# The first stage's scatter matmuls: one 128x128 matmul per slot tile instead of four in column groups of 32

## The chip, the cores and the metric

One core of one Trainium2 chip. The metric is the device time of one execution in microseconds (us). The kernel before has a median of 5328.8 us over 8 runs, from 5324.69 to 5338.14. One of its executions was profiled, and every duration below is from that execution.

## The reference, cut to what matters

A graph with 12,500 nodes of 96 features and 200,000 edges goes through four residual layers, each followed by a layer norm. The first layer is the one whose stage is changed:

```python
def _L0_gnn_ref(x, src, dst, W_self, W_neigh, b):
    n = x.shape[0]
    msg = x[src]
    neigh_sum = jax.ops.segment_sum(msg, dst, num_segments=n)
    deg = jax.ops.segment_sum(jnp.ones(src.shape, x.dtype), dst, num_segments=n)
    h_neigh = neigh_sum / jnp.maximum(deg, 1.0)[:, None]
    return x @ W_self + h_neigh @ W_neigh + b
...
x = _layernorm(x + _L0_gnn_ref(x, src, dst, L0_gnn_W_self, L0_gnn_W_neigh, L0_gnn_b), axis=-1)
x = _layernorm(x + _L1_gnn_ref(...), axis=-1)   # two rounds of the same kind of segment sum
x = _layernorm(x + _L2_gnn_ref(...), axis=-1)   # attention over the edges
x = _layernorm(x + _L3_gnn_ref(...), axis=-1)   # softmax-weighted segment sum
```

`dst` is sorted. The work that matters here is `msg = x[src]` followed by `segment_sum` over `dst`: a gather and a scatter-add.

## The kernel before, in words

Nodes are handled in 98 blocks of 128. Gather and scatter are both matmuls with one-hot matrices in fp8. For the first 76 blocks (`NS`), the edges that end in block `d` are placed in 25 *slot tiles* (`SQ`) of 128 slots. Every slot tile goes through three steps in `first_sums`:

- **gather** (L1302): four matmuls, each with 32 columns of the one-hot matrix `ohT` as weights and 192 columns of the node table (two f16 halves of 96 features) moving. Each fills one group of 32 partitions of `rows` in PSUM. They stay four in both kernels, because the four groups read different pieces of the table.
- **copy** (L1306): ScalarE turns `rows` into f16 `msg`, two or four slot tiles at a time (1 or 2 PSUM banks, alternating).
- **scatter** (L1316): `msg`, now 194 columns with a column of ones that counts the degree, is multiplied by the one-hot matrix `ohd` and added up in `acc`. 25 slot tiles end in one `acc`, which VectorE reduces (L1496).

A gather runs one group ahead of its scatter. `ohT` of a block is built from its broadcast row `bc` by VectorE (L1224) for even blocks and by ScalarE (L1221 and L1222) for odd blocks, and `ohd` by VectorE (L1206 and L1210). Both have two buffers, so those of block `d` wait until TensorE is through with block `d - 2`.

In the first stage (`passes`) this is interleaved with the bucketing of the edges (`edge_block` and `edge_steps`), which finds each edge's slot. Its steps are VectorE work (L1071 to L1087 for the counts, L1099 to L1133 for the ranks, L1142 to L1159 for the one-hot matrices `A` and `R`), with TensorE matmuls between them: L1089, L1102 and L1103, and L1166, which places 128 edges a time in `place`. ScalarE copies `place` (L1174), `expand` makes the block's rows of it (L1181, a transpose L1183, L1185), and DMAs broadcast them. The remaining 22 blocks are summed by `by_edges`, whose one-hot matrices `ones_e` (L1368) meet gathered rows in L1373. Nodes that are finished go through `l0_stage` (transposes L748, matmuls L1527).

In this stage the order of instructions on each engine is not the program's text: a scheduler sets it when the kernel is built, from what it takes each instruction to cost. Each engine then runs its own list strictly in that order. The later sums over slot tiles (`whole_pass`) have the same two steps as L1444 and L1455, and there the scatter of the second layer is one 128x128 matmul of 192 columns, while that of the fourth layer is four of 32 columns each, 384 columns long.

Of the kernel before, what the change touches and what calls it, by code (L numbers as in the profile page):

```python
# [23 lines left out]
P = 128  # L24
# [491 lines left out]
GR = 32  # L516
NG = 4
SQ = 25
# [24 lines left out]
def gnn_fast(  # L543
# [4 lines left out]
    nc = tc.nc  # L548
# [226 lines left out]
    def advance():  # L775
        if pending and next(pending[0], pending) is pending:
            pending.pop(0)
# [400 lines left out]
    def expand(work, psum, placed, d):  # L1178

        lo = work.tile([P, 2 * SQ + 1], F32, name="lo", bufs=5)  # L1180
        nc.vector.tensor_add(lo, placed[d][:, 1], placed[d + 1][:, 0])  # L1181
        p = psum.tile([SQ, P], F32, name="tp")
        nc.tensor.transpose(p, lo[:, :SQ], ident)  # L1183
        r = work.tile([SQ, P], BF16, name="lorow", bufs=2)
        nc.scalar.copy(r, p)  # L1185
        nc.scalar.dma_start(rowd[d], r)

        s = work.tile([SPARE, 1], F32, name="s_", bufs=2)
        nc.vector.scalar_tensor_tensor(
            s, lo[:SPARE, SQ : SQ + 1], float(P), lo[:SPARE, SQ - 1 : SQ], op0=ALU.mult, op1=ALU.add  # L1190
        )
        nc.vector.tensor_scalar(spare_i[:, d : d + 1], s, -1.0, 0.0, op0=ALU.add, op1=ALU.max)
        h = d % 2 * SPARE
        nc.scalar.dma_start(spare_2[h : h + SPARE, d // 2 : d // 2 + 1], spare_i[:, d : d + 1])
        return lo[:, SQ + 1 :]

    def ask_row(work, d):
        bc = work.tile([P, SD], BF16, name="bc", bufs=2)
        nc.sync.dma_start(bc, rowd[d].rearrange("q p -> (q p)")[None, :].to_broadcast([P, SD]))
        return bc  # L1200

    def destinations(work, d, lo):

        ohd = work.tile([P, SQ, P], FP8, name="ohd", bufs=2)
        by = ohd.rearrange("p q e -> p (q e)").bitcast(I32).rearrange("p (q w) -> p q w", q=SQ)
        nc.vector.scalar_tensor_tensor(  # L1206
            by, lo[:, :, None].to_broadcast([P, SQ, WQ]), 8.0, word[:, None, :].to_broadcast([P, SQ, WQ]),
            op0=ALU.mult, op1=ALU.subtract,
        )
        nc.vector.tensor_tensor(by, one8[:, None, :].to_broadcast([P, SQ, WQ]), by, op=ALU.logical_shift_left)  # L1210
        nc.sync.dma_start(ohd_d[d], ohd.rearrange("p q e -> p (q e)"))
        return ohd

    def one_hots(work, d, bc):

        o = work.tile([P, SD], FP8, name="ohT0", bufs=2)
        if d % 2:

            for c in range(0, SD, SD // 2):
                b = bc[:, c : c + SD // 2]  # L1220
                nc.scalar.activation(b, b, AF.Square, bias=less)  # L1221
                nc.scalar.activation(o[:, c : c + SD // 2], b, AF.Relu, bias=1.0, scale=-1.0, saturate=False)  # L1222
        else:
            nc.vector.tensor_scalar(o, bc, pcol1, None, op0=ALU.is_equal, saturate=False)  # L1224
        nc.sync.dma_start(ohT_d[d], o)
        return o
# [15 lines left out]
    def gather_spare(table, d):  # L1242
        ring = spare["ring"]
        t = ring[d % len(ring)]
        nc.gpsimd.indirect_dma_start(  # L1245
            out=t[:SPARE, : table.shape[1]], out_offset=None, in_=table,
            in_offset=bass.IndirectOffsetOnAxis(ap=spare_i[:, d : d + 1], axis=0),
        )
        return t
# [10 lines left out]
    def granule(at, ohs, sp, q, j, half=0):  # L1260

        if q == SQ - 1 and j < 2:
            c = half * SPARE + j * GR
            return ident_h[:, c : c + GR], sp
        s = NG * q + j - (2 if q == SQ - 1 else 0)
        return ohs[:, q * P + j * GR : q * P + (j + 1) * GR], at(s)

    AHEAD = 3
    def first_sums(work, msgp, psum, at, table, placed, done):


        W = 2 * D
        R = 2

        msgs = {}
        for banks in (1, 2):
            msgs[banks] = [msgp.tile([P, R * banks, 2, D + 1], F16, name=f"msg{banks}_{i}", bufs=1) for i in range(3)]
            for m in msgs[banks]:
                nc.gpsimd.memset(m[:, :, 0, D:], 1.0)
                nc.gpsimd.memset(m[:, :, 1, D:], 0.0)  # L1280
        got, acc, rowed, made = {}, {}, {}, {}

        def fetch(d):

            if d < NS - 2:
                made[d + 2] = expand(work, psum, placed, d + 2)
            if 0 <= d + 1 < NS:
                rowed[d + 1] = ask_row(work, d + 1)
            if 0 <= d < NS:
                got[d] = (  # L1290
                    one_hots(work, d, rowed.pop(d)), destinations(work, d, made.pop(d)), gather_spare(table, d)
                )

        def gather(now, banks):
            ps = psum.tile([P, banks, 512], F32, name=f"rows{banks}")
            m = msgs[banks].pop(0)
            msgs[banks].append(m)
            for i, (d, q) in enumerate(now):
                ohs, _, sp = got[d]
                for j in range(NG):  # L1300
                    a, b = granule(at, ohs, sp, q, j)
                    nc.tensor.matmul(  # L1302
                        ps[j * GR : (j + 1) * GR, i // R, i % R * W : (i % R + 1) * W], a, b, start=True, stop=True
                    )
            n = -(-len(now) // R)
            nc.scalar.copy(  # L1306
                m[:, : n * R].rearrange("p (b r) t w -> p b (r t) w", r=R)[:, :, :, :D],
                ps[:, :n, : R * W].rearrange("p b (t w) -> p b t w", w=D),
            )
            return [(d, q, m[:, i].rearrange("p t w -> p (t w)")) for i, (d, q) in enumerate(now)]  # L1310

        def scatter(d, q, m):
            if q == 0:
                acc[d] = psum.tile([P, 512], F32, name="acc", bufs=2)
            for j in range(0, P, GR):
                nc.tensor.matmul(  # L1316
                    acc[d][j : j + GR, : W + 2], got[d][1][:, q, j : j + GR], m, start=(q == 0), stop=(q == SQ - 1)
                )
            if q == SQ - 1:
                done(work, psum, d, acc.pop(d))  # L1320
                got.pop(d)

        for d in range(1 - AHEAD, 1):
            yield
            fetch(d)
        items = [(d, q) for d in range(NS) for q in range(SQ)]
        waiting, u, banks = [], 0, 2
        while u < len(items):
            now = items[u : u + R * banks]
            for d, q in now:  # L1330
                if q == 0:
                    yield
                    fetch(d + 1)
            waiting.append(gather(now, banks))
            u += R * banks
            banks = 3 - banks
            if len(waiting) > 1:
                for w in waiting.pop(0):
                    scatter(*w)
            advance()  # L1340
        for ws in waiting:
            for w in ws:
                scatter(*w)
# [648 lines left out]
```

## Time and profile before

| | |
|---|---|
| profiled execution | 5326.96 us; span of its instructions 5325.0 us |
| busy over the span | DVE 4158.7 us (78%), PE 4057.6 (76%), POOL 3476.8 (65%), ACT 2792.7 (52%) |
| first stage's scatters, L1316 | 7600 matmuls from 236.4 to 1270.9 us, 345.85 us busy |
| first stage's gathers, L1302 | 7600 matmuls from 230.2 to 1269.4 us |
| mean granted TensorE clock | 0.781; 0.85 in the first stage, 0.94 in the second layer's |

DVE is VectorE, ACT ScalarE, POOL GpSimd, PE TensorE, and PEld its weight loads, which lie beside the matmuls. Overlapping matmuls count once in busy time, so 7600 matmuls of 279 ns each can be busy for 345.85 us. A line such as "A L1142 <- PE place L1166" in the list of waits says that the instruction writing `A` at line 1142 stood idle until TensorE had finished an instruction that writes `place` at line 1166.

### The profile page before, as it was taken

How to read it: one execution, taken by the hardware profiler on the slowest of the kernel's cores; microseconds unless marked ns; L12 is line 12 of the kernel's file. 1: busy time of each engine (PE TensorE's matmuls, PEld its weight loads, DVE VectorE, ACT ScalarE, POOL GpSimd, SP SyncE). 2: the span in 40 equal slices, each digit the busy share in tenths (PEclk: the TensorE clock that was granted, in tenths of full speed). 3: DMA queues.
4: the chain of work that ended last, by engine and by line, in shares of the span. 5: the costliest groups of instructions: out<-in, count | busy, mean ns of one | idle time of the engine just before them, and what ended most of it. 6: DMA issues, size and time to landing. Idle time of an engine off the chain costs nothing. (4 is left out here: it accounts for less than half of the span.)

```text
span 5325.0 us, 155826 instructions
## 1 busy us (share of the span) xinstructions
PE 4057.6 (76%) x63527; PEld 3248.9 (61%) x63527; DVE 4158.7 (78%) x9827; ACT 2792.7 (52%) x5549; POOL 3476.8 (65%) x3338
## 2 busy tenths in 40 slices
PE   3677777776799889995666666766666667999997
PEld 2556666565677667774655655656656565566665
DVE  7689999994567667875888888888888887777776
ACT  1566666665455445553545455454554544555554
POOL 0276667662777477755777777777777776776661
PEclk9688888888899899995565556555565656999999
DMA  3566666656667577765555555555555554555552
GB/s 93 174 207 201 209 219 203 213 176 192 159 188 192 153 193 208 217 190 148 156 158 159 159 160 157 160 159 158 162 158 161 159 157 135 157 156 145 149 151 66
DMA packets 656950, 894.03 MB, mean 168 GB/s; under 512 B 394162, under 2 KB 458885, under 8 KB 651357
## 3 DMA queue, kind: packets, MB, share of 16 engines
q1 hardware_dynamic: 498742, 615.02, 37.1%
q0 software_dynamic: 138784, 262.63, 20.8%
q8 instruction: 500, 8.19, 0.6%
q10 hardware_dynamic: 18695, 6.32, 0.6%
q14 instruction: 229, 1.88, 0.1%
HBM read 747.72 MB, written 135.87 MB: 166 GB/s over the span
## 5 line engine op out<-in xcount | busy, mean ns | idle before, releaser
L1631 POOL DMA_INDIRECT kv<-kv_d,cols x1563 | 1548.4, 991 | 484.9 <-issue 379.0
L1389 POOL DMA_INDIRECT rows_e<-tab_d,cols x1065 | 1232.1, 1157 | 418.5 <-issue 249.6
L1447 ACT CAST msg<-rows 128x384 f16<-128x384 f32 (+1 forms) x1440 | 866.1, 641 | 637.0 <-PE rows L1444 620.5
L1725 PE MATMUL acc<-mh,ohe 128*128 128x208 f16 x2727 | 515.0, 357 | 653.7 <-DVE ohe L1709 648.7
L1447 DVE CAST msg<-rows 128x768 f16<-128x768 f32 x720 | 686.0, 953 | 331.1 <-PE rows L1444 324.8
L1444 PE MATMUL rows<-tab,ohT 128*32 128x192 f16 (+1 forms) x21560 | 796.3, 276 | 67.9 <-DVE msg L1447 35.2
L1725 PEld LDWEIGHTS <-ohe 128*128 128x128 bf16 x2727 | 306.0, 127 | 797.9 <-DVE ohe L1709 736.3
L1455 PE MATMUL acc<-msg,ohd 128*32 128x384 f16 (+1 forms) x10600 | 744.1, 300 | 7.8 <-DVE msg L1447 6.9
L1669 PE MATMUL ep<-w_e,attr 97*128 97x96 f32 x3126 | 701.8, 401 | 5.9 <-DVE s L1677 5.1
L1669 PEld LDWEIGHTS ep<-w_e,attr 97*128 97x128 f32 x3126 | 670.5, 315 | 14.4 <-DVE s L1677 5.5
L1444 PEld LDWEIGHTS <-ohT 128*32 128x32 fp8e4 x21560 | 505.5, 97 | 278.1 <-issue 204.2
L1389 POOL DMA_INDIRECT rows_e<-ex_d,cols x483 | 465.2, 963 | 203.7 <-issue 121.9
L1455 PEld LDWEIGHTS <-ohd 128*32 128x32 fp8e4 (+1 forms) x10600 | 498.5, 98 | 157.2 <-issue 74.3
L1689 ACT ACTIVATE ex<-sc 128x32 f32<-128x32 f32 x391 | 89.6, 229 | 943.4 <-DVE sc L1681 926.1
L1306 ACT CAST msg<-rows 128x768 f16<-128x768 f32 x633 | 382.0, 644 | 188.4 <-PE rows L1302 173.2
L1316 PE MATMUL acc<-msg,ohd 128*32 128x194 f16 x7600 | 345.9, 279 | 157.4 <-ACT msg L1306 155.3
L1677 DVE TENSOR_TENSOR s<-ep,kv 128x384 f32<-128x384 f32 x391 | 217.3, 556 | 317.5 <-DMA kv<-kv_d,cols 273.7
L1709 DVE TENSOR_SCALAR ohe<-wide,within 128x256 bf16<-128x256 bf16 x1563 | 361.3, 312 | 0.0
L1373 PE MATMUL acc<-rows_e,ones_e 128*128 128x192 f16 (+2 forms) x2644 | 332.1, 276 | 30.2 <-DMA rows_e<-tab_d,cols 13.1
L1316 PEld LDWEIGHTS <-ohd 128*32 128x32 fp8e4 x7600 | 209.3, 106 | 220.1 <-issue 205.3
L1302 PE MATMUL rows<-tab,ohT 128*32 128x192 f16 x7448 | 336.0, 275 | 5.4 <-issue 5.4
L1245 POOL DMA_INDIRECT spare<-tab_d,spare_i x76 | 116.0, 1527 | 327.9 <-DMA rowd<-lorow 177.2
(695 smaller groups left out, 7235.1 us busy)
## 6 DMA issues: line engine op xcount, KB each, us to landing
ohT<-ohT_d SPq DMA_DIRECT2D x220, 400.0 KB
ohd<-ohd_d SPq DMA_DIRECT2D x220, 400.0 KB
attr<-cols_edge_attr_dram SPq DMA_DIRECT2D x390, 192.0 KB
bc<-rowd SPq DMA_DIRECT2D x76, 800.0 KB
qb<-qrow SPq DMA_DIRECT2D x97, 512.0 KB
sb<-srow SPq DMA_DIRECT2D x38, 1024.0 KB
ohd_d<-ohd SPq DMA_DIRECT2D x76, 400.0 KB
ohT_d<-ohT SPq DMA_DIRECT2D x76, 400.0 KB
```

Source lines behind the costliest of these rows:

```text
L1302: nc.tensor.matmul(ps[j * GR : (j + 1) * GR, i // R, i % R * W : (i % R + 1) * W], a, b, start=True, stop=True)
L1306: nc.scalar.copy(m[:, : n * R].rearrange("p (b r) t w -> p b (r t) w", r=R)[:, :, :, :D], ps[:, :n, : R * W].rearrange("p b (t w) -> p b t ...
L1316: nc.tensor.matmul(acc[d][j : j + GR, : W + 2], got[d][1][:, q, j : j + GR], m, start=(q == 0), stop=(q == SQ - 1))
L1373: nc.tensor.matmul(acc[:, : W + count], ones[:, :, i], rows_of[u][:, t % UE + i, : W + count], start=(t + i == first), stop=(t + i == last),)
L1389: nc.gpsimd.indirect_dma_start(out=m[:, i, :W], out_offset=None, in_=table, in_offset=bass.IndirectOffsetOnAxis(ap=rest_src[:, t : t + 1], ...
L1444: nc.tensor.matmul(ps[j * GR : (j + 1) * GR, i // R, i % R * W : (i % R + 1) * W], a, b, start=True, stop=True)
L1447: (nc.scalar.copy if engine else nc.vector.tensor_copy)(m, ps[:, :, : R * W])
L1455: nc.tensor.matmul(acc[d][j : j + wide, :W], got[d][1][:, q, j : j + wide], m, start=(q == 0), stop=(q == SQ - 1))
L1631: nc.gpsimd.indirect_dma_start(out=kv[:, i, :], out_offset=None, in_=kv_d, in_offset=bass.IndirectOffsetOnAxis(ap=cols[:, t0 + i : t0 + i ...
L1669: nc.tensor.matmul(ep[:, i, :], a[:, i * P : (i + 1) * P], w_e, start=True, stop=True)
L1709: nc.vector.tensor_scalar(o[:, i], wide, within[:, t0 + i : t0 + i + 1], None, op0=ALU.is_equal)
L1725: nc.tensor.matmul(acc[d].rearrange("p t w -> p (t w)"), ohe[:, i, k * P : (k + 1) * P], m[:, i].rearrange("p t w -> p (t w)"), start=(t = ...
```

## The change

Each slot tile's four scatter matmuls, one for each group of 32 columns of `ohd`, become one matmul with all 128 columns. The operands and the sums are the same.

```diff
         def scatter(d, q, m):
             if q == 0:
                 acc[d] = psum.tile([P, 512], F32, name="acc", bufs=2)
-            for j in range(0, P, GR):
-                nc.tensor.matmul(
-                    acc[d][j : j + GR, : W + 2], got[d][1][:, q, j : j + GR], m, start=(q == 0), stop=(q == SQ - 1)
-                )
+            nc.tensor.matmul(acc[d][:, : W + 2], got[d][1][:, q, :], m, start=(q == 0), stop=(q == SQ - 1))
             if q == SQ - 1:
                 done(work, psum, d, acc.pop(d))
                 got.pop(d)
```

## The prediction

> **What bounds the kernel now.** I read the table of windows first, to find the stage that the change touches, then who waits for whom inside it, then single matmuls on the timeline. The columns of the windows are PE, PEld, DVE, ACT and POOL busy (with instructions), granted clock, DMA share and GB/s.
>
> ```profile
> core 0: us, PE busy (x) PEld busy (x) DVE busy (x) ACT busy (x) POOL busy (x), PEclk, DMA share, GB/s
> 230.00:400.00 170.00, 111.33 (x2760) 89.81 (x2758) 140.28 (x282) 104.37 (x155) 131.67 (x93) 0.80 0.69 220
> 400.00:600.00 200.00, 158.68 (x3650) 125.80 (x3651) 188.18 (x411) 133.94 (x220) 130.48 (x89) 0.88 0.65 206
> 600.00:800.00 200.00, 152.98 (x3576) 120.40 (x3569) 189.57 (x431) 128.63 (x206) 127.72 (x86) 0.85 0.66 212
> 800.00:1000.00 200.00, 153.78 (x3603) 122.21 (x3603) 189.73 (x406) 129.38 (x212) 140.46 (x86) 0.85 0.64 201
> 1000.00:1272.00 272.00, 202.12 (x4808) 161.65 (x4807) 211.13 (x473) 180.55 (x294) 130.16 (x80) 0.85 0.58 190
> ...
> 1200.00:1250.00 50.00, 35.23 (x948) 27.94 (x949) 20.13 (x41) 38.46 (x64) 6.76 (x4) 0.86 0.73 237
> ```
>
> From 400 to 1000 us DVE is busy 567.5 of 600 us, 94.6%; PE is at 77.6%, ACT at 65%. VectorE sets the pace there. From about 1200 us it does not: 20 of 50 us busy, and what is left is a tail of gathers, copies and scatters to 1271 us. So the change can act in two ways: through DVE's waits for TensorE, and through the length of the tail. Those waits, from 230 to 1200 us:
>
> ```profile
> DVE ohT L1224 <- PE rows L1302: 15.3, 8, 8.9
> DVE A L1142 <- PE place L1166: 9.4, 13, 1.8
> ...
> DVE ones_e L1368 <- PE acc L1373: 7.1, 13, 1.3
> ...
> DVE ohd L1206 <- PE acc L1316: 5.7, 5, 3.9
> ```
>
> The columns are total us, times, longest. With three smaller rows (2.3, 1.6 and twice 0.5) DVE waits 42.4 us for PE.
>
> **The matmuls themselves.** The change takes away 7600 matmuls and weight loads and adds 1900, which is certain from the built program. What array time is that? The timeline has both forms back to back: four column groups in the first stage (first two lines and the start of the third), and 128x128 scatters between 128x32 gathers in the second layer. Columns: start, us, what.
>
> ```profile
> 709.25 0.52 PE L1316 MATMUL acc<-msg,ohd 128*32 128x194 f16 x16
> 709.61 0.50 PE L1302 MATMUL rows<-tab,ohT 128*32 128x192 f16 x16
> 709.93 0.25 PE L1316 MATMUL acc<-msg,ohd 128*32 128x194 f16 x1
> ...
> 1502.16 1.01 PE L1444 MATMUL rows<-tab,ohT 128*32 128x192 f16 x40
> 1503.10 1.00 PE L1455 MATMUL acc<-msg,ohd 128*128 128x192 f16 x10
> 1504.03 0.93 PE L1444 MATMUL rows<-tab,ohT 128*32 128x192 f16 x36
> ...
> 1508.71 1.00 PE L1455 MATMUL acc<-msg,ohd 128*128 128x192 f16 x10
> 1509.54 1.32 PE L1373 MATMUL acc<-rows_e,ones_e 128*128 128x192 f16 x14
> ```
>
> Sixteen narrow scatters step in 0.36 us (709.25 to 709.61), 0.09 us a slot tile. Ten wide ones step in 0.83 us when another 128x128 matmul follows (1508.71 to 1509.54), 0.083 us a slot tile. The four narrow matmuls run side by side, so dividing the count by four saves 1900 x 0.007 = 13 us of TensorE at most; with 192 columns instead of 194 in the wide row, I take nothing. L1373 at 193 columns steps by 83 to 87 ns in this stage, which is the nearest row.
>
> **What it adds: changes of form.** The same ten wide scatters take 0.93 us when narrow gathers follow (1503.10 to 1504.03), 0.10 us more. In single records the step from one 128x128 matmul to the next is 82 ns at the median and from narrow to wide 178 ns (378 cases in the second layer; 177 to 180 in the first stage), so about 95 ns for each change. Today gathers and scatters share a form and change nothing between them. Counted in the instruction order of the two built programs between the first gather and the last scatter, TensorE changes between 128x32 and the wider forms 694 times before and 1441 times after. 747 x 0.095 = 71 us more TensorE work.
>
> The Trainium skill, TensorEngine Tiling (Array Packing), section Key Properties, speaks against the change here: changing the tiling mode drains TensorE. The trace agrees that it costs, with the 95 ns above. TensorE: Matmul & The Clock Gate, section Step-by-step, puts the pipe's drain at about 128 cycles, an estimate of 53 ns at the page's 2.4 GHz; by that the 747 changes would be 40 us instead of 71.
>
> Where does this lie? PE is busy 778.9 of 1042 us from 230 to 1272, so 263 us are free, and 71 leave 192. In the stretch set by DVE it is covered, as long as TensorE does not hold up DVE. Where PE already stands waiting for ACT's copy (155.3 us, 173 times at L1316), the pipe is empty and the change of form is likely hidden. If the cover were gone, all 71 us would show. A gain from changing form is excluded: no row has such a step below the unchanged one.
>
> **What it moves.** The instructions of DVE, ACT, POOL and SP are the same in number and kind, but the scheduler orders them otherwise in the first stage; behind it the order is the same. Three things can be counted in the lists.
>
> 1. *The tail.* After the last placement matmul (L1166), 150 slot tiles remain to be scattered before, 112 after. In the trace that matmul runs at 1209.2 us and the last scatter at 1270.9, 61.7 us for 150. At this pace 112 take 46.1: -15.6 us. In the tail each cycle of six slot tiles (a group of four and one of two) waits once through scatter, gather and copy, so one change of form lies in the chain: 112 / 6 x 0.095 = +1.8 us.
> 2. *DVE's work ahead of the tail.* What the tail lost is done earlier. With each line's mean duration, DVE has 1063.6 us of work to the end of its last L1142 before and 1070.2 after: 6.6 us more, at 94.6% busy +7.0 us.
> 3. *DVE's waits for TensorE.* Measured by placements that lie between, `ohd` of a block is asked for 5.2 tiles after its buffer is released at the mean before and 9.9 after, `ohT` 4.3 and 16. These waits (15.3 and 5.7, with 3.4 us for the row `bc`, 24.4 us) should shrink. I take half, -12 us; the ends are 0 and -24. Against it, the other waits (26 for `A` and `ones_e`, some 40 with the smaller rows and those behind `placed`) sit behind a TensorE list with more changes of form: two each are 40 x 0.19 = +8 us; the ends are 0 and the whole 71.
>
> The DMAs that DVE, POOL and SP issue move with their blocks by one block at most; the bucketing's broadcasts and the 76 indirect gathers of spare rows stay spread as they were, so I cost them at nothing. Their cover is DVE's pace; where it fails, they show as waits like `sb` on its DMA, 6.6 us in all today. TensorE's 11,400 fewer instructions (matmuls and weight loads) count for nothing either: in the first stage PE waits for "issue" 9.6 us in all, which bounds that gain.
>
> Sum: -15.6 + 1.8 + 7.0 - 12 + 8 = -10.8 us. Against the profiled execution's 5326.96 us that is 5316.2. The median of the runs is 1.8 us above that execution, so I say **5318 us**.
>
> **The rivals.**
>
> *TensorE's changes of form reach the path (slower).* In its list order TensorE delays the placements and the release of `ohT`, and DVE stands. For it: the 42.4 us that DVE waits for PE today at 78% busy, and a TensorE that goes to about 85%. Against it: 192 us still free, and many changes behind waits for ACT. Without terms for waits the sum is -6.8 us, so it decides from 17.5 us, a quarter of the 71. With half of them on the path it is -6.8 + 35.5 = +28.7, 5357 us; with all, +64, 5393 us.
>
> *DVE's waits for TensorE go altogether (much faster).* The order asks for buffers later after their release. If all 42.4 us went, the sum without the +8 is -6.8 - 42.4 = -49, 5280 us. Against it: most of these waits are short and frequent and would only pass to the next producer, ACT or a DMA.
>
> *Nothing to see.* The array time is equal, the order's effects cancel: 5322 to 5336 us. A measurement of this kernel tells about 0.2%, or 10.7 us, from no change.
>
> **How the numbers follow.** Likeliest case 0.50, with a range of its own of 5304 to 5328 us; its centre lies on the bound of 0.2%, and as the shorter tail is the firmest of the three terms I put 0.29 of it below, 0.21 within. Slower rival 0.32, of which 0.30 is over the bound and 0.02 within. Much faster 0.13. Nothing to see 0.05, of which 0.01 may be slower. So faster 0.42, same 0.27, slower 0.31. The range reaches from 5285 to 5352 us: it leaves out some 0.07 of the much faster case and 0.13 of the slower one.
>
> **What would show it.** Right: scatters at about 85 ns steps, 175 to 180 ns at each change of form, DVE at 94% or more from 400 to 1000 us, `ohT` and `ohd` waits for PE under 15 us, and the last scatter some 11 us earlier than 1270.9. The second layer, attention and fourth layer should only shift. Wrong: DVE under 93% there with longer waits of `A`, `ohT` or `ones_e` for PE (first rival), or a tail whose pace per slot tile is well over 0.41 us, or a difference that lies behind 1300 us, which nothing above would explain.

## The result and the profile after

The changed kernel takes 5350.12 us at the median (5340.66 to 5363.1, 11 runs), the kernel before 5329.04 us (31 runs): a ratio of 1.0039, interval 1.003 to 1.0048, 21 us slower. 5318 us and a gain were forecast. The time lies inside the range given, at its upper end, and on the other side of no change.

In the two profiled executions the loss is in the first stage. The last scatter ends its list at 1297.5 us instead of 1270.9, 26.6 us later; behind it they run 4053.9 us (5351.4 - 1297.5) and 4054.1 us (5325.0 - 1270.9). That these two agree so well is partly luck: over the profiled executions of all kernels here, this stretch, whose lists the change leaves alone, takes from 4047 to 4068 us. One execution therefore tells a time to some 10 us only, and the ratios below rest on many. The windows of the changed kernel, columns as before:

```profile
core 0: us, PE busy (x) PEld busy (x) DVE busy (x) ACT busy (x) POOL busy (x), PEclk, DMA share, GB/s
...
400.00:600.00 200.00, 162.55 (x2452) 108.88 (x2451) 179.16 (x405) 130.88 (x211) 132.00 (x84) 0.87 0.61 195
600.00:800.00 200.00, 160.29 (x2380) 103.89 (x2379) 181.37 (x396) 124.35 (x203) 126.99 (x85) 0.86 0.61 194
800.00:1000.00 200.00, 159.77 (x2404) 104.49 (x2397) 184.24 (x418) 125.69 (x200) 130.88 (x83) 0.86 0.64 209
1000.00:1272.00 272.00, 220.55 (x3279) 144.12 (x3275) 236.98 (x521) 185.43 (x301) 158.74 (x90) 0.87 0.64 203
1200.00:1250.00 50.00, 40.98 (x593) 26.11 (x593) 41.66 (x116) 33.84 (x63) 8.27 (x6) 0.93 0.51 168
```

From 400 to 1000 us DVE is busy 544.8 of 600 us, 90.8% instead of 94.6%. PE is at 80.4% with a third fewer instructions. From 1200 to 1250 us DVE is still at 42 of 50 us, where it had 20 before: the bucketing ends later. Over 230 to 1200 us DVE stands still 109.5 us instead of 76.5. Counted from 230 us to the end of its last `A` (L1142), VectorE's step ahead of the last placement, it stands 114.8 us instead of 76.5, 38.3 us more, and works 6.0 us more, so that this step ends at 1246.4 us instead of 1202.1. The last placement comes 0.9 us behind it instead of 7.1, at 1247.3 us instead of 1209.2: 38.1 us later. The tail behind it then takes 50.2 us instead of 61.7. 38.1 - 11.5 = 26.6 us is the whole difference.

The changed kernel's matmuls on the timeline (start, us, what, idle before):

```profile
699.91 0.50 PE L1315 MATMUL acc<-msg,ohd 128*128 128x194 f16 x4 [0.17 <-ACT msg L1306]
700.34 0.51 PE L1302 MATMUL rows<-tab,ohT 128*32 128x192 f16 x16
700.79 0.34 PE L1315 MATMUL acc<-msg,ohd 128*128 128x194 f16 x2
701.06 0.35 PE L1302 MATMUL rows<-tab,ohT 128*32 128x192 f16 x8
```

Four wide scatters and one change of form take 0.43 us (699.91 to 700.34), two take 0.27 us (700.79 to 701.06): 0.08 us for each matmul and 0.11 us for each change. In the single records of this stage the step between two wide scatters is 87 ns at the median; four narrow ones took 88 ns before. From wide to narrow it is 178 ns and from narrow to wide 179 ns, where TensorE had not stood waiting in between. These steps are as they were priced.

What VectorE waited for from 230 to 1200 us (total us, times, longest):

```profile
DVE lo L1181 <- ACT placed L1174: 14.3, 13, 2.9
DVE ss L770 <- ACT sq L767: 14.0, 9, 3.0
DVE ohd L1206 <- PE acc L1315: 13.4, 10, 5.8
DVE ohT L1224 <- PE rows L1302: 12.4, 4, 9.2
DVE ones_e L1365 <- PE acc L1370: 11.0, 13, 3.4
```

The list has another head than before. Its largest rows for ACT were these in the kernel before:

```profile
DVE to L756 <- ACT to L755: 7.7, 9, 2.1
...
DVE lo L1181 <- ACT placed L1174: 4.2, 10, 1.4
DVE ss L770 <- ACT sq L767: 3.9, 3, 1.5
```

All rows that name ACT add up to 42.7 us against 17.7. Those that name PE add up to 51.4 against 42.4. `ohd` and `ohT`, which were to shrink from 21 us to some 10, stand at 25.8.

### The profile page after: what moved, and what is told of

Read it like the earlier page. It is cut to its first block, busy times and chain, and to the rows that moved or that the text cites. A ratio compares the mean times of both kernels' runs of the same rounds, so it can differ in the third digit from the quotient of the medians.

```text
span 5351.4 us, 144372 instructions
## 1 busy us (share of the span) xinstructions
PE 4115.8 (77%) x57827; PEld 3169.7 (59%) x57827; DVE 4157.6 (78%) x9827; ACT 2797.9 (52%) x5549; POOL 3497.4 (65%) x3338
## 5 line engine op out<-in xcount | busy, mean ns | idle before, releaser
L1386 POOL DMA_INDIRECT rows_e<-tab_d,cols x1065 | 1262.2, 1185 | 404.2 <-issue 252.1
L1315 PE MATMUL acc<-msg,ohd 128*128 128x194 f16 x1900 | 306.7, 275 | 113.1 <-ACT msg L1306 104.6
L1245 POOL DMA_INDIRECT spare<-tab_d,spare_i x76 | 109.5, 1441 | 343.7 <-DVE hi_i L1012 176.2
L1670 PE MATMUL qp<-qs,ohq 128*128 128x96 f16 x3126 | 313.8, 272 | 13.6 <-DMA qs<-q_d 13.6
```

Source lines behind the costliest of these rows:

```text
L1386: nc.gpsimd.indirect_dma_start(out=m[:, i, :W], out_offset=None, in_=table, in_offset=bass.IndirectOffsetOnAxis(ap=rest_src[:, t : t + 1], ...
L1670: nc.tensor.matmul(qp[:, i, :], ohq[:, i * P : (i + 1) * P], qs[:, t * D : (t + 1) * D], start=(t == 0), stop=(t == 1))
```

## The experiments

The change does two things at once: it makes TensorE change form more often, and it makes the scheduler write other lists. To have one without the other, the lists were pinned: a chain of issue-order edges on each engine holds a list that another kernel's build made. The edges carry no wait for a semaphore (`NoSync`) and add no instruction: in the traces VectorE runs the same sequence of instructions in the kernel before and in the wide kernel that is held in its lists. The code is shortened here. Each run has its own measurement of the kernel before beside it, which is why that median differs a little from run to run.

```diff
+    for e, text in ORDER.items():          # one list per engine, from the other kernel's build
+        order = decoded(text)
+        for a, b in zip(order, order[1:]):
+            tc.add_manual_dep(made[e][b], made[e][a].name, NoSync, reason="pinned")
```

### One without the other

Wide scatters in the old lists:

> The wide scatters of the changed kernel, with every engine's list held in the order of the kernel before (a wide matmul stands where the last of its four narrow ones stood). TensorE changes form 1407 times in the first stage, against 694 before and 1441 in the changed kernel. Theory A, changes of form: nearly all of the loss is here, +15 to +30 us on the kernel before, DVE's waits for PE from 230 to 1200 us go from 42 us to 60 or more, and the last scatter is 15 us or more later than 1271 us. Theory B, the scheduler's new order: 0 to +6 us, DVE at 94% from 400 to 1000 us as before, last scatter within 6 us of 1271.

Narrow scatters in the new lists:

> The four narrow scatters of the kernel before, with every engine's list held in the order of the changed kernel. TensorE changes form 650 times in the first stage. Theory A, changes of form: without them the new order gives what its shorter tail was priced at, -5 to -15 us on the kernel before. Theory B, the scheduler's new order: +15 to +25 us as in the changed kernel, DVE near 91% from 400 to 1000 us with its waits for ACT (row copies, squares, transposed halves) at some 40 us from 230 to 1200 us, against 18 before.

Measured: wide in the old order 1.0036 (1.0023 to 1.0049), 5352.8 against 5335.7 us. Narrow in the new order 1.0027 (1.0016 to 1.0038), 5352.1 against 5335.7. By the ratios that is +19 us and +14 us (+17 and +16 by the medians). So there was a loss in each kernel: the changes of form in the first, the lists in the second, each near what its theory said. Not all of it came as written: VectorE's waits for PE in the first kernel stopped at 53.1 us, short of 60, and 14 us lies just under the 15 that the second theory began with. Taken by itself each half of the change costs 14 to 19 us, and both together cost 21, not 33; with intervals of 5 to 7 us to either side, the gap between 21 and 33 is just clear of the noise. DVE's waits from 230 to 1200 us, first wide in the old order:

```profile
DVE ohT L1224 <- PE rows L1302: 16.6, 7, 10.2
DVE to L756 <- ACT to L755: 12.3, 12, 1.9
DVE ones_e L1365 <- PE acc L1370: 11.0, 15, 1.6
DVE ohd L1206 <- PE acc L1315: 8.9, 7, 5.8
```

and narrow in the new order:

```profile
DVE ss L770 <- ACT sq L767: 13.7, 9, 2.7
DVE ohd L1206 <- PE acc L1316: 13.3, 11, 5.8
DVE ohT L1224 <- PE rows L1302: 11.8, 4, 9.2
DVE ones_e L1368 <- PE acc L1373: 11.7, 16, 3.2
DVE lo L1181 <- ACT placed L1174: 11.5, 13, 2.2
```

In the old order with wide scatters the same rows lead as in the kernel before, each a little longer: `ohT` 15.3 to 16.6, `to` 7.7 to 12.3, `ones_e` 7.1 to 11.0, `ohd` 5.7 to 8.9. The rows with PE rise from 42.4 to 53.1 us in all, and DVE stands 93.1 us. In the new order with narrow scatters, `ss` and `lo` are at the top as in the changed kernel: that signature comes with the lists, not with the wide matmuls. Here DVE stands 101.2 us, and the tail takes 48.6 us: the shorter tail is had, and DVE's standing and the work moved ahead of the tail take more than it gives. The rows with PE stand at 50.7 us, and at 51.4 in the changed kernel. So the second half of the change found these waits already long. That this is why the two do not add is a reading of single executions, not shown by a run of its own.

A difference in the clock does not explain these losses: the mean granted clock over all executions is 0.773 in the first of the two kernels and 0.777 in the second, against 0.776 for the kernel before beside them. Over 79 executions of the kernel before, the clock ran from 0.768 to 0.784, and the time did not go with it.

### How much a change of form costs

In the old order, 269 runs of scatters and the gathers behind them changed places in TensorE's list, so that two groups are gathered and then two scattered:

```diff
 TensorE's list, groups k to k+2
-gather k+1, scatter k, gather k+2, scatter k+1
+gather k+1, gather k+2, scatter k, scatter k+1
```

> Wide scatters in the order of the kernel before, with one edit to TensorE's list: at 269 places where the scatters of one group stand directly ahead of the gathers of the next, the two runs change places, so that two groups are gathered and then two are scattered. TensorE changes form 919 times in the first stage instead of 1407 (694 before). If changes of form cost what they cost in the wide kernel of the old order (+19 us for 713 extra), the 225 extra here cost +6 us; bounds +2 to +10 us. If the loss there comes from the wide matmul itself or from its place in the list, +15 to +22 us stay.

The same exchange with narrow scatters as a control:

> Control for the wide kernel with paired groups: narrow scatters in the old order, with the same 269 exchanges in TensorE's list, 690 changes of form. If the exchange itself is neutral, -3 to +3 us on the kernel before, and what pairing won back with wide scatters was the changes of form. If the exchange helps by itself, -6 us or more.

Measured: wide and paired 1.0011 (1.0002 to 1.002), +6 us; the control 1.0003 (0.9993 to 1.0014). The exchange by itself is neutral, and it took the wide kernel of the old order from +19 to +6 us. The first stage has 694 changes of form in the kernel before, 1407 with wide scatters in the old order and 919 after the exchange: 713 extra changes for 19 us and 225 for 6 us are both some 27 ns for each, against the 95 ns that a change was priced at on TensorE: 28% of it reaches the end. By the intervals it is 17 to 37 ns in the first kernel and 5 to 47 ns in the second, so that the two agree so closely is partly luck. The wide matmul itself costs nothing that can be seen within some 6 us. In DVE's waits the lengthened rows go back:

```profile
DVE ohT L1224 <- PE rows L1302: 16.0, 7, 10.2
DVE to L756 <- ACT to L755: 9.2, 9, 1.9
...
DVE ohd L1206 <- PE acc L1315: 7.3, 11, 3.0
...
DVE ones_e L1365 <- PE acc L1370: 4.2, 8, 1.1
```

DVE stands 78.3 us here, the rows with PE are at 40.7. This profile is of the fastest of the run's 11 executions, 5324.8 us against a median of 5335.4, so it shows somewhat shorter waits than the usual one. In the new order the same exchange was tried:

> The changed kernel with 257 such exchanges in TensorE's list: 959 changes of form instead of 1441. With the old order's price (19 us for 713) it falls from +21 to +8 us on the kernel before; with the price that the two kernels of the new order show (6 us for 791) to +17 us. In no case below +5 us, since the order's own loss of some 14 us stays.

Measured 1.0038 (1.0025 to 1.0051), 5343.9 against 5328.0 us; the changed kernel has 1.0039. A third of its changes of form away, and no gain that can be told: in this order they are not what holds it.

### What is wrong with the new order

Was the old order merely a lucky one? Two kernels scatter a single block wide, which adds only 16 and 26 changes of form but makes the scheduler write new lists:

```diff
+            wide = P if d == 1 else GR      # the other kernel: d == 3
+            for j in range(0, P, wide):
```

> Only the 25 slot tiles of block 1 are scattered with wide matmuls, all others as before, and the scheduler orders the stage anew: from there on its lists differ (of 1921 VectorE instructions in the differing stretch 913 stand in the old sequence), while TensorE changes form 710 times against 694, worth 0.4 us at the old order's price. If the order of the kernel before is a favourable one among those the scheduler makes, +6 to +20 us on the kernel before. If only the order made for mostly wide scatters is slow, -4 to +4 us; a longer tail (178 slot tiles after the last placement, not 150) may add some 8 us to either.

> The same with block 3 alone: 720 changes of form (0.7 us), 597 of 1882 VectorE instructions in the old sequence, and 150 slot tiles in the tail as before. Favourable-order theory: +6 to +20 us. The other: -4 to +4 us.

Measured 1.0003 (0.9994 to 1.0012) and 1.0013 (1.0004 to 1.0021), +1 and +7 us. These lists differ from the old ones about as much as the changed kernel's do: in the stretch of VectorE's list that differs, 1113 of 1921 and 1102 of 1882 instructions still follow each other in the old sequence, and 1129 of 1984 in the changed kernel. (This is counted alike for all three from the traces, where an instruction is known by its line, shape and place among its like; the expectations counted more strictly.) So a different list need not cost much. But +7 us lies in the range written down for a favourable old order, and none of the new orders was faster than the old one: that the old order is simply a good draw is not excluded. The first kernel has 178 slot tiles in its tail, and its median shows no loss by it. Then narrow scatters in the lists made for a kernel in which every second block is wide:

> Narrow scatters in the order that the scheduler makes when every second block is scattered wide; 686 changes of form. If an order gets worse the more of the scatters it takes to be cheap, +5 to +10 us on the kernel before, between the old order (0) and the new (+14). If the loss belongs to the one order of the changed kernel, it lies with the two orders that one wide block made (+1 and +6 us): 0 to +6 us; over +10 us would say that most of the loss comes with the first cheap scatters.

1.0037 (1.0023 to 1.005), +20 us, with 5 runs: the loss is there in full with half of the scatters taken to be cheap. The long waits for ACT are not: VectorE waits 18.5 us for it in this kernel's profile, with `ss` at 3.7 and `lo` at 3.5, as in the kernel before. That profile is of the fastest of the five executions, 5334.9 us, so it can't say where the rest of the loss lies.

Last, VectorE's list was edited: where it stood still in the trace, the waiting instruction was put behind later ones that do not depend on it. In three kernels that was done at nearly all places:

```diff
 VectorE's list, X waits for another engine, Y and Z do not depend on X
-X, Y, Z
+Y, Z, X
```

> The kernel before with its VectorE list alone edited: at 75 of the 82 places where VectorE stood still for 0.2 us or more between 230 and 1260 us of the profiled execution, the waiting instruction is put behind the next ones that do not depend on it (137 instructions go ahead, worth 60.8 of 106.9 us of standing). If the standing is a matter of the order in the list, -15 to -45 us on the kernel before; if the engines that VectorE waits for set the pace, the waits return elsewhere and the time stays within 8 us.

> Narrow scatters in the changed kernel's order, with the same edit of the VectorE list from this kernel's own trace (94 of 100 places, 199 instructions go ahead, 82.7 of 113.7 us). If the new order is slow because it puts VectorE instructions close behind their producers, the kernel falls from +14 us to between -15 and -40 us on the kernel before, as the shorter tail is then kept. If the order is slow for another reason, it stays at +10 to +18 us.

> The changed kernel with the same edit of its VectorE list (93 of 97 places, 205 instructions go ahead, 87.3 of 116.4 us). Order theory: from +21 us to -10 to -35 us on the kernel before. If changes of form hold the kernel, it gains 10 us at most and stays slower than the kernel before.

Measured 1.005 (1.0037 to 1.0063), 1.0064 (1.0052 to 1.0076) and 1.0093 (1.0079 to 1.0108): +27, +34 and +50 us. Against the lists that were edited (0, +14 and +21 us), the edit costs 27, 20 and 29 us. Both outcomes written down beforehand for these kernels were wrong. DVE's standing was not filled: in the first it grew from 76.5 to 95.5 us, and the waits moved (all engines' list from 230 to 1200 us, a row of TensorE's and one of VectorE's):

```profile
PE pr L1089 <- DVE sb L1087: 31.1, 16, 10.1
DVE ohd L1206 <- PE acc L1316: 28.3, 15, 8.4
```

Before, these rows had 23.8 and 5.7 us. The likely reason, which no run isolates, is that a step that VectorE waits for is often one that other engines wait for next, and that work put ahead of it delays them. So the edit was narrowed to steps of the node stage, which no bucketing waits for:

> Narrow scatters in the changed kernel's order, with VectorE's list edited only where it stood for a step of the node stage that follows the sums (its squares, roots, transposed halves and reductions; 27 places, 28.2 us): these steps go behind bucketing instructions that do not depend on them (63 go ahead). The earlier edit also moved bucketing steps, which others wait for. If the new order is slow because steps of the node stage stand in front of bucketing steps and are not ready, it falls from +14 us to -12 to +2 us on the kernel before. If the place of these steps does not matter, +10 to +18 us stay.

> The kernel before with the same kind of edit (17 places, 16.1 us, 32 instructions go ahead). If such steps in front of bucketing steps cost their standing time, -6 to -16 us on the kernel before; if other waits take their place, -3 to +4 us.

Measured 1.0021 (1.0012 to 1.003) in the new order, where it had been 1.0027 (1.0016 to 1.0038), and 1.002 (1.001 to 1.003) in the old, +11 us each. In the new order the two intervals overlap, and the edit did not bring it back, as the second outcome had it; in the old order it costs, which neither outcome had. In the new order the row of `ss` is gone, where it led with 13.7 us, and VectorE waits 24.9 us for ACT instead of 36.7. Yet the rows with PE rose from 50.7 to 57.4 us, and DVE stands 98.1 us instead of 101.2: more than half of what left one producer came back at another.

What makes the new lists slow stays open. It is in the lists. The long waits for ScalarE go with the changed kernel's lists, but edits that took away a fifth to two fifths of them (36.7 to 29.2 and 24.9 us, 42.7 to 26.1) did not take away the loss, and the profile of the lists for every second block does not have them. They are a mark of these lists and not shown to be the cause. No kernel tried here beats the one before.

## Why the prediction was wrong

**Right.** The array time: four narrow matmuls step by 88 ns and one wide one by 87 ns in this stage, so the smaller count brought nothing. The price and number of the changes of form: 91 to 92 ns above that step in the changed kernel, 95 forecast. The Trainium skill, TensorEngine Tiling (Array Packing), section Key Properties, says that a change of mode drains TensorE; the trace agrees in so far as a change costs time, 91 to 92 ns. The 53 ns estimated from TensorE: Matmul & The Clock Gate, section Step-by-step, is too low as its price. The work ahead of the tail: +6.6 us were forecast, +6.9 came from the start to the last `A`. The tail: 47.9 us were forecast for its 112 slot tiles (46.1 at the old pace and 1.8 for changes of form), 50.2 came. That the later layers only shift, too.

**Wrong: the third term, -12 + 8 us.** It had two parts, and both failed.

- The waits of `ohT` and `ohd` were to fall by half because the lists ask for these tiles more placements after their release. They went from 21.0 to 25.8 us, and in the new order without wide matmuls to 25.1. The number of placements between release and use did not tell how long they wait; and counting looked only at two rows that led the list before, not at those that would lead it after. `ss` and `lo` brought 20 us that no step of the sum had.
- The changes of form were given 8 us by way of some 40 waits at two changes each. In the old order, where they can be seen alone, they cost 19 us (12 to 26). The slower rival put its turning point at a quarter of the 71 us; 28% was measured there, just beyond it and not told from it by the interval. It was the right mechanism for that kernel, and it was given 0.32.

In the changed kernel the order alone would have been enough: narrow scatters in its lists lose 14 us. The rival that failed most clearly is the much faster one, where VectorE's waits for TensorE go: they grew to 51.4 us. The term missing from the sum was the whole of what a new order does to waits that it does not share with the old one, and no bound was set on it above zero. In all, the two parts stood for -4 us of VectorE's standing, and to the last `A` it rose by 38.3 us. That the measured time still lies inside the range, at its upper end, is owed to the width that the slower rival gave it, and not to the likeliest case.

## What to carry to other kernels

Where a scheduler writes the lists, a change of one instruction's apparent cost is two changes, and pinning one kernel's lists to the other's instructions tells them apart in two runs. Before widening a column-tiled matmul (one that uses a group of 32 columns) that alternates with tiled ones, count the changes of form in TensorE's list and group the runs: with the old lists, pairing two groups won back 13 of 19 us, and with the new lists nothing that could be told. A wait on the busiest engine is not spare room: putting ready work ahead of the waiting step cost 20 to 29 us in three kernels here.

## What the runs showed of the hardware

A change between the 128x32 and 128x128 form takes TensorE 91 to 92 ns beyond the 87 ns step, in both directions. With the old lists TensorE was busy 83% from 400 to 1000 us, VectorE 93%, and about 27 ns of each change (17 to 37) still reached the end. That some 28% of a price comes through on an engine that had 263 us to spare before was not expected.
